# Query products of a two-layer kernel as three rounded passes of exact parts, with the heads of both sequences walked together

## The chip, the core and the metric

The kernel runs on one core of one Trainium2 chip. The metric is the device time of one execution in microseconds. The times shown are the median of three executions with the lowest and the highest beside it; the profile is of one execution.

## What is computed

Two layers, each an attention part and a feed-forward part, each followed by a residual sum and a layernorm. The change lies in the attention part of the first layer, a linear attention that reads a fixed memory, and in the way the weights of the first feed-forward part are examined. Cut to that:

```python
# x: (2, 512, 512); of the 32 heads only every 4th is used: 8 heads of 128 columns
q      = elu(x @ Wq.T + bq) + 1.0            # (b, s, 8, 128) for the 8 heads
num    = einsum('bshd,hde->bshe', q, M)      # M: (8, 128, 128)
den    = einsum('bshd,hd->bsh', q, z) + 1e-6
out    = repeat(num / den, 4 heads) @ Wo.T
x      = layernorm(x + out)
# first feed-forward: weights are ternary (-s, 0, +s), results are truncated to int8
gate, up = (x / 128) @ w_gate.T, (x / 128) @ w_up.T      # 1376 columns each
inter  = trunc(clip(silu(gate) * up * 128, -128, 127))
x      = layernorm(x + trunc(clip((inter @ w_down.T) * 128, -128, 127)))
# then a softmax attention with one head and a SwiGLU feed-forward, both untouched here
```

## The kernel before, in words

Everything lies in one function, `tile_two_layers_kernel`. A sequence of 512 rows is held as 4 row tiles of 128 x 512 (`xs[b][t]`). A scheduling layer places the instructions of TensorE (PE), VectorE (DVE), ScalarE (ACT) and the SyncE DMA queue (SP) from the program's order and its own costs; GpSimd (POOL) keeps the written order. `tc.issue_after` ties one instruction behind another. PSUM is one pool of 8 tiles of one bank each (`ps`, L68); tiles of a pool with `bufs=n` are reused in turn, and a new user waits for the readers of the old one.

**Query stage.** `transposed` (L117) and `first_rows` (L358) turn the rows with PE transposes and copy them to SBUF as `xt`. For each sequence b and head h, `queries` (L379) makes `q`: `query_products` (L350) runs 4 float32 products of 128 x 128 weights with 128 x 512 rows into one bank, ACT makes `e` (Exp, L388) and `r` (Relu, L390) from it, and DVE joins them to `q` (L392). Only head 0 of sequence 0 is done in quarters of 128 columns, as its rows arrive. All heads of sequence 0 come first, then all heads of sequence 1. Between them lie `sum_weights` (L404: three additions of output weights, on POOL for heads 0, 3, 5, 7, on DVE for the others) and `fold` (L412), which multiplies M with the summed output weights into `mw`, 128 x 512 a head; its last column is z (the denominator).

**Reading stage.** For each of the 8 row tiles, `read` (L419) runs 8 float32 products of `q` with `mw` into 8 banks (L428). ACT takes the denominators (L432), DVE inverts four at a time (L436), ACT scales three heads to `y` (L441), POOL adds them up (L445, L457), and DVE adds the other five heads to the rows (L450). `norm_a0` (L526) is the layernorm.

**Checks.** Whether the first feed-forward's weights are ternary is found out on the chip. `largest`, `over_partitions` and `scales` (L178 to L206) find the scale of gate and up from the first chunk. `check_up` (L469) divides a half chunk (128 x 512, 22 halves in 11 chunks) by the scale on ACT (L463) and compares it with the original on DVE (L210, one instruction and a read of its accumulator), counting the differences. 15 halves are checked from head 3 of sequence 1 on, 7 in the first three row tiles of the reading. `divided` (L537) runs the same division again, into tiles that the feed-forward keeps (`ts_up`), for the first `LEAD` = 6 chunks in the reading's last six row tiles. `total` and `verdict` (L214, L219) give one flag and the scale to use, `branch` (L234) loads the flag into PE registers, and `up` (L604) branches on it: 16 fp32r products per chunk and sequence (L611), with rows in two parts.

**Loads.** SP issues x of sequence 0, the query weights, x of sequence 1, M, the output weights, and then all gate and up chunks (`up_weights`, L237); `wo` tiles come from a pool of 6, so their loads wait for `sum_weights`.

The function that makes exact parts elsewhere in the kernel, in the last feed-forward:

```python
h = w * (1 - 2**-13)            # rounded to fp32r by ACT (L803)
l = (h * -4096) + 4096 * w      # DVE (L817)
d = l - h                       # DVE (L818)
```

Of the kernel before, what the change touches and what calls it, by code (L numbers as in the profile page):

```python
# [32 lines left out]
LENT = 3  # L33
TOP12 = -4096
# [4 lines left out]
def kernel(  # L39
# [179 lines left out]
    def verdict(tot, sc, name):  # L219

        k = sc.shape[-1]
        pf = psum(f"pf_{name}")
        nc.tensor.matmul(pf[:, :1], ones, tot, start=True, stop=True)
        yes = small.tile([P, 1], F32, tag="yes", name=f"yes_{name}", bufs=1)
        nc.vector.tensor_scalar(yes, pf[:, :1], 0.0, None, ALU.is_equal)
        no = small.tile([P, 1], F32, tag="no", name=f"no_{name}", bufs=1)
        nc.vector.tensor_scalar(no, pf[:, :1], 0.0, None, ALU.not_equal)
        flag = const.tile([1, 1], I32, tag=f"flag_{name}", name=f"flag_{name}")
        nc.vector.tensor_copy(flag, yes[0:1, 0:1])
        eff = const.tile([P, k], F32, tag=f"eff_{name}", name=f"eff_{name}")  # L230
        nc.vector.tensor_scalar(eff, sc, yes, no, ALU.mult, ALU.add)
        return flag, eff
# [69 lines left out]

    wqp = ctx.enter_context(tc.tile_pool(name="wqp", bufs=4))

    def query_tile(name):
        return wqp.tile([P, 2, HID], F32, tag="wq", name=name)

    with tc.tile_pool(name="a0w", bufs=1) as a0w, tc.tile_pool(name="a0", bufs=2) as a0:
# [12 lines left out]
        load_x(1)  # L321
# [4 lines left out]
        for h in range(NH):  # L326
            halves = []
            if h == 6:
                gus = up_weights(gu0_in, "0", range(1))
            for j in range(2):  # L330
                w = pair_tile(f"wo{h}_{j}")
                nc.sync.dma_start(w, wo0_in[h, :, ts(j, G // 2), :])
                halves.append(w)
            wos.append(halves)

        gus += up_weights(gu0_in, "0", range(1, len(CHUNKS)))
        nc.sync.dma_start(wqkv, wqkv_in.rearrange("(k p) f -> p k f", p=P))
        bqk = const.tile([D, 3], F32, tag="bqk", name="bqk")
        nc.sync.dma_start(bqk, bqk_in)
        nc.sync.dma_start(bv, bv_in.to_broadcast([P, D]))  # L340
        nc.sync.dma_start(wo1, wo1_in)
        nc.sync.dma_start(bo, bo_in.to_broadcast([P, HID]))

        mw = a0w.tile([D, NH, HID], F32, tag="mw", name="mw")
        nc.gpsimd.tensor_copy(mw[:, :, LAST], z)

        def query_products(pq, xt, h, at):  # L350
            for k in range(NK):
                done = nc.tensor.matmul(  # L352
                    pq[:, at], wq[h][:, k, :], xt[:, k, at],
                    start=(k == 0), stop=(k == NK - 1),
                )
            return done

        def first_rows(xt, t):  # L358

            pt = psum(f"pt_a00_{t}")  # L360
            for k in range(NK):
                done = nc.tensor.transpose(pt[:, ts(k, P)], xs[0][t][:, ts(k, P)], ident)
            pt = pt.rearrange("p (k t) -> p k t", k=NK)
            nc.scalar.copy(xt[:, :2, ts(t, P)], pt[:, :2])
            nc.vector.tensor_copy(xt[:, 2:, ts(t, P)], pt[:, 2:])
            return done

        def first_queries(pq, xt):

            done = first_rows(xt, 0)  # L370
            for t in range(NT):
                if t + 1 < NT:
                    with tc.issue_after(done.ins):
                        done = first_rows(xt, t + 1)
                with tc.issue_after(done.ins):
                    done = query_products(pq, xt, 0, ts(t, P))
            return done

        def queries(b, xt, h):  # L379

            pq = psum(f"pq_{b}_{h}")
            if b == h == 0:
                done = first_queries(pq, xt)
            else:
                done = query_products(pq, xt, h, slice(0, S))

            e = a0.tile([D, S], F32, tag="e", name=f"e_{b}_{h}")
            nc.scalar.activation(e, pq, AF.Exp, bias=bq[:, h : h + 1])  # L388
            r = a0.tile([D, S], F32, tag="r", name=f"r_{b}_{h}")
            nc.scalar.activation(r, pq, AF.Relu, bias=bq[:, h : h + 1])  # L390
            q = a0.tile([D, S], F32, tag="q", name=f"q_{b}_{h}", bufs=16)
            nc.vector.scalar_tensor_tensor(q, e, 1.0, r, ALU.min, ALU.add)  # L392
            qs[b].append(q)
            return done
# [65 lines left out]
        def ternary(eng, out, w, factor):  # L460

            if eng is nc.scalar:
                eng.activation(out, w, AF.Copy, scale=factor)  # L463
            else:
                eng.tensor_scalar(out, w, factor, None, ALU.mult)  # L465

        counts = const.tile([P, 2 * len(CHUNKS)], F32, tag="counts", name="counts")

        def check_up(c, a):  # L469
            n = CHUNKS[c][1]  # L470
            w = gus[c][:, a].rearrange("p k i -> p (k i)")
            t = a0.tile([P, NK * P], F32R, tag="t", name=f"t_{c}_{a}")
            ternary(nc.scalar, t[:, : NK * n], w, inv_up[:, a : a + 1])
            junk = a0.tile([P, NK * P], I8, tag="junk", name=f"junk_{c}_{a}", bufs=1)
            i = 2 * c + a
            compare(
                junk[:, : NK * n], t[:, : NK * n].bitcast(F32), w,
                sc_up[:, a : a + 1], counts[:, i : i + 1],
            )

        checks = [(c, a) for c in range(len(CHUNKS)) for a in range(2)]
        qs = [[], []]
        xt = xtp.tile([P, NK, S], F32, tag="xt", name="xt_a00")
        with tc.issue_after(queries(0, xt, 0).ins):
            queries(0, xt, 1)
        for h in range(2, NH):
            queries(0, xt, h)
            if h == 4:
                sum_weights(nc.gpsimd, 0)
                turn_memory()  # L490
                sum_weights(nc.vector, 1)
            elif h == 6:
                xt1 = transposed(xs[1], "a01")
                sum_weights(nc.vector, 2)
        sum_weights(nc.gpsimd, 3)
        for h in range(NH):
            queries(1, xt1, h)
            if h == 0:
# [4 lines left out]
                with tc.issue_after(copies[-1].ins):  # L503
                    mx_up = largest(
                        [gus[0][:, a].rearrange("p k i -> p (k i)") for a in range(2)], "up"
                    )
            elif h == 1:
                top_up = over_partitions(mx_up, "up")
            elif h == 2:
                sc_up, inv_up = scales(top_up, "up")  # L510
                fold(2)
# [3 lines left out]
            elif h == 3:  # L515
                fold(4)
            elif h == 5:
                fold(5)
                fold(6)
            elif h == 6:  # L520
                fold(7)
            if h >= 3:
                for _ in range(3):
                    check_up(*checks.pop(0))
        order = [(b, t) for b in range(B) for t in range(NT)]
        def norm_a0(i, steps):  # L526
# [10 lines left out]
        def divided(c, a):  # L537
            n = CHUNKS[c][1]
            if c not in ts_up:
                t = (pair_tile if c in PAIRED else query_tile)(f"tu_{c}").bitcast(F32R)  # L540
                ts_up[c] = t.rearrange("p a (k i) -> p a k i", k=NK)
                if n < P:
                    nc.gpsimd.memset(ts_up[c][:, :, :, n:].bitcast(F32), 0.0)
            ternary(nc.scalar, ts_up[c][:, a, :, :n], gus[c][:, a], inv_up[:, a : a + 1])

        PAIRED = (LEAD - 2, LEAD - 1, len(CHUNKS) - 1)
        ts_up, x2 = {}, []
# [5 lines left out]
        for i, (b, t) in enumerate(order):  # L553
            steps = read(b, t, lambda steps: norm_a0(i - 1, steps) if i else None)
            for _ in range((3, 2, 2, 0, 0, 0, 0, 0)[i]):
                check_up(*checks.pop(0))
            if i == 3:
                tot_up = total(counts, "up")
            elif i == 4:
                flag_up, eff_up = verdict(tot_up, sc_up, "up")  # L560
            if i >= len(order) - LEAD:
                for a in range(2):
                    divided(i - len(order) + LEAD, a)
# [30 lines left out]
    with tc.tile_pool(name="f0", bufs=2) as f0:  # L594
        ternary_up = branch(flag_up)
        silu_scale = const.tile([P, 1], F32, tag="silu_scale", name="silu_scale")
        nc.vector.tensor_scalar(silu_scale, eff_up[:, 0:1], 1.0 / 128.0, None, ALU.mult)
# [6 lines left out]
        def up(b, c, behind=()):  # L604
            n = CHUNKS[c][1]
            t = ts_up[c]
            pp = [psum(f"pg_f0{b}_{c}"), psum(f"pu_f0{b}_{c}")]
# [110 lines left out]

        for c in range(LEAD - 2):
            up(0, c, [cut_off[f"f00_{c - 2}"]] if c > 1 else ())  # L720
        parts, block = split(1, xt1)
# [75 lines left out]
    BIG = 4096.0  # L797
    MAIN, CROSS = 1.0 + 1.0 / BIG, 1.0 / BIG
    UPPER = 1.0 - 2.0**-13
# [34 lines left out]

    def units(tile):
        return [tile[:, i, :] for i in range(tile.shape[1])]
# [484 lines left out]
```

## Time and profile before

| what | value |
|---|---|
| time, median of 3 (lowest to highest) | 471.77 us (470.95 to 472.08) |
| profiled execution, first to last instruction (span) | 468.7 us; the page prints no other time of its own for it |
| instructions | 5727 |
| PE busy | 461.0 us (98%) |
| DVE busy | 329.5 us (70%) |
| ACT busy | 267.5 us (57%) |
| POOL busy | 115.1 us (25%) |
| granted PE clock | 0.998 |
| query stage on PE, first query product to first reading product | 6.15 to 72.32 us |
| reading stage on PE, to the first product of the feed-forward | 72.32 to 130.65 us |

How to read it: a busy PE is not a PE at its peak, since the matmuls are pipelined and their ends are modelled; the distance between the starts of equal instructions is the better measure of what one costs. A line such as `L428` is the line of the kernel. "Idle before" is the time that an engine stood still before the instructions of a group, and the name after the arrow is what ended that time.[...]

### The profile page before, as it was taken

The page shows a single profiled execution, that of the slowest core. Times are in us where ns is not written, and L with a number is a line of the kernel's source. Part 1 is how long each engine was busy: PE and PEld are TensorE (multiplying, and loading weights), DVE is VectorE, ACT ScalarE, POOL GpSimd, SP SyncE. Part 2 cuts the span into 40 slices and gives each one's busy share as a digit, 9 for nine tenths or more (in the row PEclk, how much of TensorE's full clock was granted, in tenths as well). Part 3 has the DMA queues.
Part 4 walks back from the last instruction along what each step waited for, and adds up shares of the span by engine and source line. Part 5 has one row for each costly group of instructions (what it writes and reads, how often), then busy time and mean ns, then how long its engine had stood idle before and what let it go on. Part 6 is the DMA issues. An engine that isn't in the chain of part 4 may idle for free.

```text
span 468.7 us, 5727 instructions
## 1 busy us (share of the span) xinstructions
PE 461.0 (98%) x1883; PEld 329.0 (70%) x1883; DVE 329.5 (70%) x627; ACT 267.5 (57%) x507; POOL 115.1 (25%) x144
## 2 busy tenths in 40 slices
PE   9999999999999999999999999999999999999994
PEld 8454444434478888888866567888888888888884
DVE  1165677767876767775979889895755778998632
ACT  3344799557756767456756842584645768443101
POOL 0235101566543053600357032000000000050111
PEclk9999999999999999999999999999999999999999
DMA  8989900000006500051390000000000000001001
GB/s 284 381 297 363 387 9 0 0 0 3 1 1 134 201 1 3 11 162 45 91 390 31 0 1 1 1 0 1 1 0 1 0 1 1 1 24 45 37 31 45
DMA packets 21651, 35.02 MB, mean 75 GB/s; under 512 B 9840, under 2 KB 10736, under 8 KB 21616
## 3 DMA queue, kind: packets, MB, share of 16 engines
q1 hardware_dynamic: 19616, 33.73, 20.7%
q10 hardware_dynamic: 1872, 0.56, 0.5%
q8 instruction: 22, 0.36, 0.3%
q0 software_dynamic: 128, 0.26, 0.3%
q14 instruction: 13, 0.11, 0.1%
HBM read 31.40 MB, written 2.10 MB: 71 GB/s over the span
## 4 chain that ended last, share of the span: by engine, by line
PE 71%; ACT 7%; DVE 5%; issue 3%; POOL 0%; POOLq 0%; DVEq 0%; ACTq 0%
PE pm L1111 17%; PE pg_f L611 9%; PE pu_f L611 9%; PE pc L1111 8%; PE pdm L1199 7%; PE pd_f L666 4%; PE pdc L1199 4%; DVE x L450 3%; PE pqk L893 3%; PE po L428 2%; ACT y L441 2%; ACT t L463 2%; PE pv L906 2%; PE pot L989 1%; PE po L1005 1%
## 5 line engine op out<-in xcount | busy, mean ns | idle before, releaser
L428 PE MATMUL po<-mw,q 128*128 128x512 f32 x128 | 57.1, 598 | 0.3 <-DVE mv_a L139 0.2
L352 PE MATMUL pq<-xt_a,wq 128*128 128x512 f32 (+1 forms) x152 | 56.9, 526 | 0.0
L145 POOL TENSOR_TENSOR rstd_f<-mv_f,ln_eps 128x1 f32<-128x1 f32 x15 | 4.4, 293 | 169.3 <-DVE mv_f L1214 130.2
L428 PEld LDWEIGHTS po<-mw,q 128*128 128x128 f32 x128 | 22.9, 189 | 32.1 <-issue 17.7
L352 PEld LDWEIGHTS pq<-xt_a,wq 128*128 128x128 f32 x152 | 26.2, 190 | 27.4 <-issue 25.7
L1111 PE MATMUL pm<-r,ugu 128*128 128x512 f32 x152 | 37.7, 389 | 0.0
L1111 PE MATMUL pm<-r,it_early 128*128 128x512 f32 x144 | 36.7, 392 | 0.0
L1111 PEld LDWEIGHTS pm<-r,ugu 128*128 128x128 f32 x152 | 28.5, 188 | 5.9
L1111 PEld LDWEIGHTS pm<-r,it_early 128*128 128x128 f32 x144 | 27.0, 188 | 6.1 <-issue 0.5
L169 ACT ACTIVATE ta_f<-y_f,below_half 128x512 int8<-128x512 f32 (+1 forms) x22 | 15.9, 721 | 27.0 <-DVE y_f L157 26.7
L450 DVE SCALAR_TENSOR_TENSOR x<-po,den,x 128x511 f32<-128x511 f32 x40 | 29.8, 745 | 1.9
L1121 DVE SCALAR_TENSOR_TENSOR ev_q<-pm,ev_q 128x512 f32<-128x512 f32 x27 | 18.6, 688 | 14.4 <-PE pm L1111 14.4
L637 DVE SCALAR_TENSOR_TENSOR it_f<-tb_f,ta_f 128x512 fp32r<-128x512 int16 (+1 forms) x22 | 15.4, 702 | 18.3 <-ACT tb_f L170 18.3
L445 POOL TENSOR_TENSOR y<-y,y 128x511 f32<-128x511 f32 x16 | 20.3, 1271 | 31.5 <-ACT y L441 30.8
L388 ACT ACTIVATE e<-pq,bq 128x512 f32<-128x512 f32 x16 | 11.1, 692 | 24.1 <-PE pq L352 20.6
L611 PE MATMUL pg_f<-xh,tu 128*128 128x512 f32 x88 | 24.3, 398 | 0.0
L1120 ACT ACTIVATE ev_q<-pc 128x512 f32<-128x512 f32 x27 | 16.0, 593 | 14.2 <-PE pc L1111 14.1
L465 POOL TENSOR_SCALAR td<-wd,inv_down 128x512 fp32r<-128x512 f32 x11 | 18.2, 1668 | 22.1 <-DVE inv_down L205 22.1
L611 PE MATMUL pg_f<-xl,tu 128*128 128x512 f32 x88 | 23.6, 390 | 0.0
L611 PE MATMUL pu_f<-xh,tu 128*128 128x512 f32 x88 | 23.5, 389 | 0.0
L611 PE MATMUL pu_f<-xl,tu 128*128 128x512 f32 x88 | 23.5, 389 | 0.0
L1001 ACT ACTIVATE x<-x,off_f,rstd_f 128x512 f32<-128x512 f32 x7 | 5.7, 816 | 27.7 <-POOL off_f L1000 27.7
(315 smaller groups left out, 1087.5 us busy)
## 6 DMA issues: line engine op xcount, KB each, us to landing
gu<-in_gu SPq DMA_DIRECT2D x20, 512.0 KB, 7.9
wo<-in_wo SPq DMA_DIRECT2D x16, 512.0 KB, 6.9
wd<-in_wd SPq DMA_DIRECT2D x20, 256.0 KB, 4.5
wq<-in_wq SPq DMA_DIRECT2D x8, 256.0 KB, 4.9
x<-in_x SPq DMA_DIRECT2D x7, 256.0 KB, 5.4
out<-x SPq DMA_DIRECT2D x7, 256.0 KB, 2.0
wqkv<-in_wqkv SPq DMA_DIRECT2D x1, 768.0 KB, 10.8
xt_f<-squares SPq DMA_DIRECT2D x9, 64.0 KB, 2.4
```

The source lines that it names most:

```text
L169: nc.scalar.activation(a[:n], y, AF.Relu, bias=below_half[:n])
L352: done = nc.tensor.matmul(pq[:, at], wq[h][:, k, :], xt[:, k, at], start=(k == 0), stop=(k == NK - 1),)
L428: nc.tensor.matmul(po, qs[b][h0 + j][:, ts(t, P)], mw[:, h0 + j, :], start=True, stop=True,)
L445: nc.gpsimd.tensor_add(ys[0][:, :LAST], ys[0][:, :LAST], y[:, :LAST])
L450: steps.append(nc.vector.scalar_tensor_tensor(x[:, :LAST], four[j][:, :LAST], d, x[:, :LAST], ALU.mult, ALU.add))
L465: eng.tensor_scalar(out, w, factor, None, ALU.mult)
L611: nc.tensor.matmul(pp[a], t[:, a, i % NK, :], x2[b][i], start=(i == 0), stop=(i == 2 * NK - 1),)
L666: nc.tensor.matmul(pd, inter[b][c][:, ts(t, P)], td[c].bitcast(F32R), start=(c == 0), stop=(c == last),)
L1111: nc.tensor.matmul(p, w, x, start=(left[id(p)] == begun[id(p)]), stop=(left[id(p)] == 1))
L1120: nc.scalar.activation(ev, pc, AF.Copy, scale=CROSS)
L1121: nc.vector.scalar_tensor_tensor(ev, pm, MAIN, ev, ALU.mult, ALU.add)
L1199: nc.tensor.matmul(p[:, :w], got[j // 4][1][kind][:, j % 4], down_parts[j][kind][:, cols], start=(j == 0 and kind == kinds[0]), stop=(j == ...
```

## The change

1. **Query products in parts.** The weights of a head are cut into `g`, `l`, `d` (`exact_weights`: one ACT and two DVE instructions of 128 x 512), the rows into an upper part `h`, a remainder `m` and a cross part `d` (`upper_lower`: one ACT, one DVE; `crossed`: one DVE). Instead of 4 float32 products a head takes 12 fp32r products into one bank: 8 (`g` with `h`, `l` with `m`), then ACT multiplies the bank in place by 4097 (`raise_main`), then 4 more (`d` with `d`) are added onto it. The bank then goes to Exp and Relu as before. Head 0 of sequence 0 keeps its float32 quarters; its rows are copied for that and cut into parts besides.
2. **Both sequences together.** After head 0 of sequence 0 come heads 1, 2, 3 of sequence 0, then 1, 2, 3, 0 of sequence 1, then heads 4 to 7, each for both sequences. The main passes of an item are issued ahead of the cross pass of the item before it.
3. **Room.** The parts lie in tiles of other things: the buffers of the gate and up chunks 2 to 10 (`hosts`), of `y`, `t` and three of the four `wos`. So the loads of these chunks, and the five small loads behind them, are written after the query stage (`late_loads`); chunks 0 and 1 (`EARLY` = 2) are loaded ahead of the output weights of the last heads. x of sequence 1 is loaded after the third head's weights.
4. **Checks in the reading.** Four halves are checked in the query stage, 18 with the reading. For the first 6 chunks the check uses the division that `divided` keeps, so that these 12 halves are divided once and not twice.
5. **Two verdicts.** Chunks 0 to 5 are counted for one flag, 6 to 10 for a second one (`up2`), which is made between the feed-forward's third and fourth chunk.

```diff
+    def exact_weights(w, parts):
+        g, l, d = parts
+        nc.scalar.activation(g, w, AF.Copy, scale=UPPER / BIG)
+        nc.vector.scalar_tensor_tensor(l, g.bitcast(F32), -BIG, w, ALU.mult, ALU.add)
+        nc.vector.tensor_sub(d, l.bitcast(F32), g.bitcast(F32))
+    def upper_lower(src, h, m):
+        return (
+            nc.scalar.activation(h, src, AF.Copy, scale=UPPER),
+            nc.vector.tensor_sub(m, src, h.bitcast(F32)),
+        )
+    def crossed(d, h, m):
+        return nc.vector.scalar_tensor_tensor(
+            d, m.bitcast(F32), -BIG, h.bitcast(F32), ALU.mult, ALU.add
+        )
+    def raise_main(p):
+        return nc.scalar.activation(p, p, AF.Copy, scale=BIG + 1.0)
...
-        gus += up_weights(gu0_in, "0", range(1, len(CHUNKS)))
-        nc.sync.dma_start(wqkv, wqkv_in.rearrange("(k p) f -> p k f", p=P))
+        def late_loads():
+            gus.extend(up_weights(gu0_in, "0", range(EARLY, len(CHUNKS))))
+            nc.sync.dma_start(wqkv, wqkv_in.rearrange("(k p) f -> p k f", p=P))
...
+            lows.append(upper_lower(pt, high0[:, :, ts(t, P)], low0[:, :, ts(t, P)]))
...
+        def passes(p, b, h, kinds, start):
+            todo = [(wq3[h][i][:, ts(k, D)], rows3[b][i][k]) for i in kinds for k in range(NK)]
+            for i, (w, x) in enumerate(todo):
+                done = nc.tensor.matmul(
+                    p, w, x, start=(start and i == 0), stop=(i == len(todo) - 1),
+                    skip_group_check=not start,
+                )
...
+        def main_queries(b, h):
             pq = psum(f"pq_{b}_{h}")
-            if b == h == 0:
-                done = first_queries(pq, xt)
-            else:
-                done = query_products(pq, xt, h, slice(0, S))
+            passes(pq, b, h, (0, 1), True)
+            raise_main(pq)
+            return b, h, pq
+        def cross_queries(b, h, pq):
+            if (b, h) != (0, 0):
+                passes(pq, b, h, (2,), False)
             e = a0.tile([D, S], F32, tag="e", name=f"e_{b}_{h}")
...
+        for i, (b, h) in enumerate(items):
+            begun = main_queries(b, h)
...
+            cross_queries(*held)
+            held = begun
...
+            if i > len(items) - 3:
+                for _ in range(2):
                     check_up(*checks.pop(0))
+        fold(7)
+        cross_queries(*held)
+        late_loads()
...
-            for _ in range((3, 2, 2, 0, 0, 0, 0, 0)[i]):
+            for _ in range((1, 2, 2, 3, 3, 2, 3, 2)[i]):
                 check_up(*checks.pop(0))
-            if i >= len(order) - LEAD:
-                for a in range(2):
-                    divided(i - len(order) + LEAD, a)
...
+        tot_up = total(counts_up[1], "up2")
         for c in range(LEAD - 2):
             up(0, c, [cut_off[f"f00_{c - 2}"]] if c > 1 else ())
+            if c == 2:
+                decide(1, *verdict(tot_up, sc_up, "up2"))
```

In the built program the scheduling layer moves the checks of the reading forward: all 18 comparisons stand on DVE in the first four row tiles, and five divisions of chunks 2 to 4 stand on ACT ahead of the first `y`. SP issues chunk 5 first of the late loads, then 2, 3, 4 and 6 to 10. The second flag's product stands on PE behind the feed-forward's third chunk, and its load into registers behind the fourth.

## The prediction

> **What bounds the kernel now.** I read, in this order: engine totals, busy time by stretch, the order of time on each engine, the waits. Totals and stretches (start:end, length, then busy time of each engine, instruction count in brackets, then granted clock, DMA share, GB/s):
>
> ```profile
> PE 461.0 (98%) x1883; PEld 329.0 (70%) x1883; DVE 329.5 (70%) x627; ACT 267.5 (57%) x507; POOL 115.1 (25%) x144
> 24.00:41.00 17.00, 17.00 (x59) 8.99 (x58) 11.47 (x16) 6.98 (x12) 6.43 (x4) 1.00 0.92 324
> 56.00:72.30 16.30, 16.30 (x39) 7.22 (x38) 11.62 (x28) 16.30 (x32) 0.00 (x0) 1.00 0.17 57
> 93.00:99.90 6.90, 6.90 (x17) 2.77 (x16) 4.30 (x11) 3.81 (x14) 4.13 (x6) 1.00 0.00 0
> ```
>
> PE never rests: the query stage (6.15 to 72.32) and the reading (72.32 to 130.65) are its work. ACT is full from 56 to 72, with checks. In a row tile of the reading (6.9 us) DVE is busy 4.3, POOL 4.1. The order of time (start, length, instruction) prices single steps by the distance of starts:
>
> ```profile
> 14.35 0.69 ACT L388 ACTIVATE e<-pq,bq 128x512 f32<-128x512 f32 x1 [2.17 <-PE pq L352]
> 17.78 0.69 ACT L388 ACTIVATE e<-pq,bq 128x512 f32<-128x512 f32 x1 [2.17 <-PE pq L352]
> 131.98 1.09 PE L611 MATMUL pg_f<-xl,tu 128*128 128x512 f32 x4
> 132.91 1.07 PE L611 MATMUL pu_f<-xh,tu 128*128 128x512 f32 x4
> 27.51 0.68 DVE L392 SCALAR_TENSOR_TENSOR q<-e,r 128x512 f32<-128x512 f32 x1
> 28.12 0.68 DVE L409 TENSOR_TENSOR wos<-wo 128x512 f32<-128x512 f32 x1
> ```
>
> A head of 4 float32 products comes every 3.43 us, 0.857 a product. Four fp32r products take 0.907 (131.98 to 132.89), 0.227 each. A DVE pass of 128 x 512 takes 0.60, an ACT one 0.58 from PSUM (0.61 from SBUF). DVE beside POOL:
>
> ```profile
> 248.92 1.65 DVE L818 TENSOR_TENSOR it_early<-it_early 128x512 fp32r<-128x512 f32 x1
> 243.31 11.73 POOL L967 TENSOR_TENSOR x<-x,bo 128x512 f32<-128x512 f32 x8
> 267.94 0.69 DVE L818 TENSOR_TENSOR ugu<-ugu,ugu 128x512 fp32r<-128x512 f32 x1
> 52.27 1.76 DVE L210 SCALAR_TENSOR_TENSOR junk<-t,sc_up,gu 128x512 int8<-128x512 f32 x1
> 52.03 1.45 POOL L409 TENSOR_TENSOR wos<-wo 128x512 f32<-128x512 f32 x1 [5.43 <-PE pmw L414]
> 54.16 0.75 DVE L210 SCALAR_TENSOR_TENSOR junk<-t,sc_up,gu 128x512 int8<-128x512 f32 x1
> ```
>
> The same subtraction takes 0.69 alone and 1.65 while POOL adds; the comparison 0.75 and 1.76.
>
> [...] the blocked DVE step ends about 0.5 us behind POOL's. The DVE sum L450, which has one input in PSUM, keeps to 0.73 to 0.75 throughout, POOL busy or not. [...] The trace: 0.857 / 0.227 = 3.8. [...]
>
> **The change part by part.** R is the start of the reading on PE, 72.32 before.
>
> *PE, query stage.* 15 heads go from 3.43 to 12 x 0.227 = 2.72 us: -0.71 x 15 = -10.65, so R = 61.7 if nothing waits. Transposes and folds are the same in number.
>
> *ACT, query stage.* Added: 15 raises x 0.58 = 8.7; 8 weight cuts x 0.61 = 4.9; uppers 4 x 0.6 = 2.4 for sequence 0, for sequence 1 two more passes than the two copies they replace, 1.2. Sum +17.2. Gone: 17 of the 21 divisions before 72.3, -10.4. With 16 x (0.58 x 2) = 18.6 for e and r, 8 folds x 0.78 = 6.2, 2.5 of copies and the four remaining divisions, ACT has some 48 us of work in the 55 between 6 and 61: hidden. PE needs a raise only behind the next head's eight products (1.8 us), and ACT needs about 1 for it. An in-place pass in PSUM is not shown; nearest row L1120 (PSUM to SBUF, 0.59). From 0.5 to 0.7 it stays hidden; I take 0.58.
>
> *DVE, query stage.* Added: 16 weight passes, 8 cross parts, 4 remainders and 2 net for sequence 1, 30 x 0.60 = 18; gone 12 comparisons x 0.85 = 10.2. Sum +7.8, to about 44 us in 55. But it is crowded at the start. First rows: the copies that the float32 quarters wait for now stand behind two uppers and a weight cut on ACT (1.8 us, where ACT idled 1.2 and 1.0 ahead of these copies) and behind two remainders on DVE. Walking both queues with these durations, the first fp32r product starts at about 11.8, where head 1 started at 10.4: +1.4 us. Lower bound 0.5 (weights of head 1 land early and all is hidden), upper 2.5. From there to 24 us DVE has no gap: what it makes there, weight parts, cross parts and the remainders of sequence 1, PE takes at once.
>
> *POOL against DVE there.* POOL's first summing began at 20.5, when its weights had landed; the loads ahead of it hold the same bytes, so it begins there again, 2.35 + 1.26 us. In it DVE has two-SBUF passes that PE waits for. DVE loses up to 3.6; some of it is spent in remainders, which read PSUM, and the PE queue has about 1 us in hand: +1.8, bounds 0 and 3.6. Later sums (10.9 us of POOL) meet a DVE with about 13 us free: nothing. R = 61.7 + 1.4 + 1.8 = 64.9.
>
> *Reading.* PE alone needs 64 x 0.857 + 16 transposes (1.9) + 0.2 = 57.0; before took 58.3. DVE per row tile: 5 x 0.66 + 0.6 + two inversions and small ones 0.6 = 4.5. The 18 comparisons x 0.85 now all stand in the first four tiles, 11 us of them (13 comparisons) in tiles 1 to 3 and the end of tile 0. DVE then needs 10.5, 7.8, 7.9, 6.0 us, against 6.9 of PE. POOL reads SBUF 4.1 us of 6.9, and blocks a comparison until its addition ends: walked through, about eight of the 18 are caught, 0.2 to 1.1 us each, 3.5 in all. The bank of head 7 of tile t is needed by head 7 of tile t+1, which PE reaches at R + 12.9, 19.9, 26.8, 33.7; DVE frees it at R + 14.6, 23.2, 31.7, 39.1. So PE loses up to 39.3 - 33.7 = 5.6 us by tile 4; behind that DVE needs less than PE. 57.0 + 5.6 = 62.6, with 0.4 for other short stops 63.0: +4.7 on before's 58.3. Without the blocking 2.5, with every comparison caught in full 8.
>
> *Late loads.* Chunks 2 to 10 (4.6 MB) leave the query stage, whose DMA was never the bound. Chunk 2's tile comes free when the cross pass of (0, 7) is done, R - 1.8. A 256 KB load into an idle queue took 3.0; 256 KB more at the 391 GB/s of the page add 0.7: an estimate of 3.7, so R + 2.0. ACT's first division, queued ahead of three denominators and all y, has its turn at R + 2. Nothing more is lost, but there is no cover: every microsecond of lateness moves y, and the bank of head 0 has only half a microsecond.
>
> *ACT in the reading.* 3.6 us a tile, 18 divisions x 0.61 = 11, four casts: some 43 in 63. The 10 divisions of `divided` that stood in the reading go; they were under PE.
>
> *Second verdict.* One product of one column (0.14 on PE), one register load (0.1 at the flag of down, 204.64) behind a further 3.6 us of products, five small DVE steps under PE: +0.2. The remainder of the kernel is as it was, shifted.
>
> Sum: -10.65 + 1.4 + 1.8 + 4.7 + 0.2 = -2.6 us. The two walks lean to the late side: the scheduler's order lets POOL wait for DVE as well as DVE for POOL, and I charged DVE every time. I take 0.6 off and predict -3.2. The span is 468.7, to 465.5. The median lies 3.1 above that span; I keep this: 468.6.
>
> **The rivals.** (1) *DVE keeps up*: comparisons slip between POOL's additions, start hidden by half. -10.65 + 0.7 + 0.6 + 1.5 + 0.2 = -7.6, 464.1. For it: the L450 passes are never blocked, DVE was 62% busy in a tile. Against: 11 us of comparisons against three tiles with 2.4 us free each. (2) *No change*: the upper ends of start and blocking, -10.65 + 2 + 2.5 + 5.5 + 0.2 = -0.5, 471.3. (3) *Slower: the late loads hold ACT.* In the reading's first tile five divisions stand in ACT's queue ahead of the first y. If chunk 2 lands at R + 8, as loads did in the full queue of before (7.9 us median from issue), and the others 1.3 us apart, y, the denominators and through them all DVE sums start 6 us later, in front of DVE's full three tiles: -3.2 + 6 = +2.8, 474.6. It decides from about 3.2 us of lateness. Against: the queue is empty then. (4) The change does not do what it says, the fp32r passes costing more with changing weights: L611 changes weights at every product too, so I give it nothing.
>
> **How the numbers follow.** About 0.3%, 1.4 us, is what a measurement of this kernel can tell from no change. My case, -1.4 to -5.5: 0.42. Rival 1: 0.30. Rival 2: 0.16. Rival 3: 0.12. Faster 0.72, same 0.16, slower 0.12. The range: 463.3 (below rival 1 by 0.8) to 472.2 (above rival 2 by 0.9) leaves out rival 3 and a little at the low end.
>
> **What would show it.** Right: first fp32r product near 11.8; the reading starting at 63.5 to 66; comparisons of 1.0 to 1.8 us under POOL's additions in tiles 1 to 3; reading products waiting for DVE sums there, none after tile 4; 62 to 64 us of reading. Wrong: a gap on ACT ahead of the first division (rival 3), a reading of 59 us (rival 1), raises that PE waits for late in the query stage, or a start of the reading behind 68.

## The result, and the profile after

The changed kernel took 474.37 us (median of 7 runs, 471.96 to 474.64), the kernel before 470.95 beside it (7 runs, 470.31 to 472.08): a ratio of 1.0056, 95% interval 1.0037 to 1.0074. It is slower by half a per cent. 468.6 was predicted, in a range up to 472.2. The profiled execution is one of the quick ones: span 470.5, its own time 472.3.

The totals first, then two stretches of the changed kernel (start:end, length, busy time and instruction count of PE, PE's weight loads, DVE, ACT, POOL; then granted clock, DMA share, GB/s) that answer to those shown of before:

```profile
PE 455.3 (97%) x1945; PEld 341.9 (73%) x1945; DVE 358.7 (76%) x663; ACT 277.2 (59%) x524; POOL 127.3 (27%) x144
```

```profile
24.00:41.00 17.00, 17.00 (x77) 13.45 (x77) 15.37 (x18) 11.48 (x20) 6.41 (x3) 1.00 0.70 245
93.00:99.90 6.90, 5.91 (x13) 2.00 (x12) 6.69 (x17) 4.66 (x14) 4.10 (x4) 1.00 0.00 0
```

PE is busy for 5.7 us less, and no longer all of it back to back: in the row tile of the reading at 93 it stands for a seventh of the time, and DVE is full. The larger hole lies in the query stage. PE in order of time there (start, length, instruction; in brackets how long it stood still before it, and what ended that):

```profile
32.65 1.07 PE L502 MATMUL pq<-xh_a,host_t 128*128 128x512 f32 x4
33.55 1.07 PE L502 MATMUL pq<-xl_a,host_t 128*128 128x512 f32 x4
34.46 1.07 PE L502 MATMUL pq<-host,host_y 128*128 128x512 f32 x4
35.37 1.98 PE L502 MATMUL pq<-host,host_t 128*128 128x512 f32 x8
...
43.14 3.33 PE L502 MATMUL pq<-host,host_y 128*128 128x512 f32 x12
50.05 0.38 PE L202 MATMUL pbc_up<-dg_up,ones 2*128 2x2 f32 x2 [3.58 <-DVE dg_up L195]
...
50.92 2.01 PE L502 MATMUL pq<-xh_a,host_t 128*128 128x512 f32 x4
52.73 1.91 PE L502 MATMUL pq<-xl_a,host_t 128*128 128x512 f32 x4
```

Twelve fp32r products come in 2.7 us from start to start, as reckoned (32.65 to 35.37). At 46.47 PE falls idle and stands for 3.58 us in front of a product of two columns: the one that spreads the checks' scale over the partitions. Behind the stop four products take 1.8 us from start to start, twice their 0.91: the granted clock fell.

```profile
46.50:50.00 3.50, 0.00 (x0) 0.00 (x0) 3.46 (x7) 2.36 (x5) 0.16 (x1) 1.00 0.93 266
50.00:52.00 2.00, 1.95 (x7) 1.31 (x8) 1.97 (x6) 0.48 (x2) 1.83 (x1) 0.91 1.04 364
52.00:54.00 2.00, 2.00 (x6) 1.53 (x5) 2.00 (x2) 1.90 (x3) 2.00 (x1) 0.50 0.24 94
54.00:56.00 2.00, 2.00 (x7) 1.52 (x6) 2.00 (x2) 1.33 (x4) 1.66 (x2) 0.73 0.00 0
```

The low clock costs 2 x (0.09 + 0.50 + 0.27) = 1.7 us. What PE waits for is the scale's second small step, `dg_up`. DVE ahead of it:

```profile
42.64 2.87 DVE L317 SCALAR_TENSOR_TENSOR host_t<-host_t,wq 128x512 fp32r<-128x512 f32 x1
45.58 2.17 DVE L538 TENSOR_TENSOR wo<-wo,wo 128x1024 f32<-128x1024 f32 x1
47.67 0.68 DVE L540 TENSOR_TENSOR wos<-wo 128x512 f32<-128x512 f32 x1
...
48.87 0.68 DVE L318 TENSOR_TENSOR host<-host_t,host_t 128x512 fp32r<-128x512 f32 x1
49.47 0.27 DVE L193 TENSOR_REDUCE top_up<-pmx_up 2x1 f32<-2x128 f32 x1
49.78 0.22 DVE L195 TENSOR_SCALAR dg_up<-ident,top_up 2x2 f32<-2x2 f32 x1
```

A weight step that takes 0.6 elsewhere took 2.87, a sum of output weights 2.17 where others took 1.2. POOL in the same time:

```profile
42.20 2.76 POOL L538 TENSOR_TENSOR wo<-wo,wo 128x1024 f32<-128x1024 f32 x1 [5.28 <-DVE host_y L318]
45.04 1.62 POOL L540 TENSOR_TENSOR wos<-wo 128x512 f32<-128x512 f32 x1
```

The weight step (42.64 to 45.51) ends half a microsecond behind POOL's sum (42.20 to 44.96), and the next DVE sum ends behind POOL's next one (45.04 to 46.66): these two DVE steps lost 2.3 + 1.0 us, about what PE stood still. It is the taking of turns that the prediction's pairs from the kernel before show (a subtraction of 0.69 and 1.65 us, a comparison of 0.75 and 1.76), at a place where it had charged nothing.

So the reading starts at 68.31, not at 64.9 (before 72.32). It takes 62.99 us, and 63.0 were predicted. One more wait, of 0.94 us, lies far behind: a layernorm step ahead of the last transposes (234.10), behind two small steps of POOL for it that took 2.08 and 1.48 instead of 0.55. It is in this profile only; the others of this document don't show it.

### The profile page after: what moved, and what is told of

It reads as the page before. It is cut to its first block, busy times and chain, and to the rows that moved or that the text cites. A ratio compares the mean times of both kernels' runs of the same rounds, so it can differ in the third digit from the quotient of the medians.

```text
span 470.5 us, 5923 instructions
## 1 busy us (share of the span) xinstructions
PE 455.3 (97%) x1945; PEld 341.9 (73%) x1945; DVE 358.7 (76%) x663; ACT 277.2 (59%) x524; POOL 127.3 (27%) x144
## 4 chain that ended last, share of the span: by engine, by line
PE 68%; DVE 5%; issue 2%; POOL 1%; ACT 1%; POOLq 0%; DVEq 0%
PE pm L1242 17%; PE pg_f L744 9%; PE pu_f L744 8%; PE pc L1242 8%; PE pdm L1330 7%; PE pdc L1330 4%; PE pqk L1024 3%; PE po L559 3%; DVE x L581 2%; PE pv L1037 2%; PE pot L1120 1%; PE po L1136 1%; PE psc L1062 1%; PE pd_f L799 1%; POOL rstd_f L146 1%
## 5 line engine op out<-in xcount | busy, mean ns | idle before, releaser
L559 PE MATMUL po<-mw,q 128*128 128x512 f32 x128 | 58.8, 603 | 3.2 <-DVE x L581 1.9
L146 POOL TENSOR_TENSOR rstd_f<-mv_f,ln_eps 128x1 f32<-128x1 f32 x15 | 6.9, 458 | 168.1 <-DVE mv_f L1345 130.3
L576 POOL TENSOR_TENSOR y<-y,y 128x511 f32<-128x511 f32 x16 | 22.8, 1427 | 22.3 <-ACT y L572 21.7
L538 POOL TENSOR_TENSOR wo<-wo,wo 128x1024 f32<-128x1024 f32 x4 | 15.4, 3849 | 21.5 <-DVE q L524 6.4
L524 DVE SCALAR_TENSOR_TENSOR q<-e,r 128x512 f32<-128x512 f32 x16 | 14.5, 906 | 8.2 <-ACT r L522 8.2
L799 PE MATMUL pd_f<-td,it_f 128*128 128x512 f32 x88 | 20.3, 389 | 0.0
```

The lines of the kernel that those rows point to most:

```text
L559: nc.tensor.matmul(po, qs[b][h0 + j][:, ts(t, P)], mw[:, h0 + j, :], start=True, stop=True,)
L576: nc.gpsimd.tensor_add(ys[0][:, :LAST], ys[0][:, :LAST], y[:, :LAST])
L799: nc.tensor.matmul(pd, inter[b][c][:, ts(t, P)], td[c].bitcast(F32R), start=(c == 0), stop=(c == last),)
```

## The experiments

The profiled execution of each (start and length of the reading are PE's; a ratio is to the kernel before in the same runs):

| run | stop at the scale, us | reading starts | reading takes | span | median of runs | ratio, 95% interval |
|---|---|---|---|---|---|---|
| before | none | 72.3 | 58.3 | 468.7 | 470.95 | |
| as changed | 3.58 | 68.3 | 63.0 | 470.5 | 474.37 | 1.0056 (1.0037 to 1.0074) |
| e1_scale_later | 2.84 | 67.6 | 63.0 | 468.7 | 470.77 | 1.0005 (0.9991 to 1.0018) |
| e2_no_pool | none | 63.1 | 63.1 | 464.1 | 466.01 | 0.9903 (0.9889 to 0.9917) |
| e3_no_cmp | 3.65 | 68.4 | 58.8 | 465.4 | 467.75 | 0.9959 (0.9940 to 0.9978) |
| e4_spread | 5.73 | 71.5 | 61.7 | 473.5 | 474.35 | 1.0068 (1.0056 to 1.0081) |
| e5_sums_dve | none | 62.5 | 62.6 | 462.9 | 465.88 | 0.9911 (0.9898 to 0.9923) |
| e6_no_y_adds | 5.66 | 70.8 | 58.0 | 466.6 | 468.54 | 0.9964 (0.9952 to 0.9977) |
| e7_scale_first | 3.63 | 68.3 | 62.9 | 469.4 | 471.48 | 1.0038 (1.0025 to 1.0050) |
| e8_dve_spread | none | 62.7 | 64.4 | 464.8 | 466.85 | 0.9922 (0.9908 to 0.9935) |
| c1_before_dve | none | 72.3 | 58.0 | 468.5 | 470.67 | 1.0003 (0.9995 to 1.0012) |
| e11_both | none | 63.5 | 58.6 | 459.9 | 461.08 | 0.9791 (0.9775 to 0.9807) |
| e10_lent2 | none | 63.0 | 60.3 | 461.1 | 462.85 | 0.9836 (0.9822 to 0.9849) |
| c2_after_again | 3.70 | 68.4 | 62.7 | 469.3 | 472.91 | 1.0050 (1.0037 to 1.0064) |
| e12_sum_first | 5.92 | 71.2 | 63.9 | 472.8 | 474.09 | 1.0071 (1.0058 to 1.0085) |

### The stop in the query stage

**Put the scale's product later.**

```diff
             elif i == 9:
-                top_up = over_partitions(mx_up, "up")
                 fold(2)
             elif i == 10:
-                sc_up, inv_up = scales(top_up, "up")
                 fold(3)
...
             elif i == 11:
+                top_up = over_partitions(mx_up, "up")
                 fold(4)
             elif i == 12:
+                sc_up, inv_up = scales(top_up, "up")
                 fold(5)
```

> Only the place of the scale chain changes: its transpose stands two items later in the query stage, its product (the one that PE waited 3.58 us for at 46.5) two items later too. Main theory (this one product, standing in PE's order in front of work that was ready, holds PE while DVE is late, and the rest of the loss is the lower granted clock of 0.5 to 0.9 from 50 to 56, which costs 1.7 and comes only from the stop): no stop at 46.5, clock 1.00 up to 60, the reading starts at 63.0 (62.5 to 64) instead of 68.3, time about 469.0. Rival A (the stop alone goes, the low clock has another cause): start 64.7, slow products still near 51. Rival B (another DVE product takes its place, since DVE stays as late as it is): a stop of 2 to 3.5 us before weights or folded sums between 45 and 52, start 66 to 68, time 472 or more.

PE of this kernel, in order of time:

```profile
52.87 0.85 PE L502 MATMUL pq<-host,host 128*128 128x512 f32 x3
56.55 0.35 PE L202 MATMUL pbc_up<-dg_up,ones 2*128 2x2 f32 x2 [2.84 <-DVE dg_up L195]
...
57.40 2.31 PE L502 MATMUL pq<-xh_a,host_y 128*128 128x512 f32 x4
```

The stop at 46.5 went, and came again at 53.7, under the same product, with the same slow products behind it; the start moved by 0.8 only. PE worked from 46.5 to 53.7 on products that in the changed kernel stood behind this one: there, ready work waited behind a product that could not start. POOL's next sum (49.93 to 52.52, and 1.6 of its second part) stretched the two DVE steps ahead of the scale there as well. So the main theory was wrong in taking this product's place for the cause; it was right about the clock, which fell where the stop was. Rival B is near in the start (66 to 68), not in the time: 470.77, where it had 472 or more. It is DVE's lateness that has to go.

**Take POOL's sums away.** Part of the computation is left out, as the expectation says.

```diff
             w, w1 = wos[h]
-            eng.tensor_add(w, w, w1)
             s = a0.tile([D, HID], F32, tag="wos", name=f"wos{h}", bufs=4)
+            if eng is nc.gpsimd:
+                nc.scalar.copy(s, w[:, 0, :])
+                nc.scalar.copy(s[:, :1], w1[:, 0, :1])
+                wos[h] = s
+                return
+            eng.tensor_add(w, w, w1)
             eng.tensor_add(s, w[:, 0, :], w[:, 1, :])
```

> Leaves out POOL's additions of the output weights of heads 0, 3, 5 and 7: ACT copies the first of the four blocks instead (0.6 us each), so nothing reads SBUF on POOL in the query stage; the order on DVE and PE stays. Main theory (POOL's two-input additions and DVE's two-input steps take turns on SBUF and stretch each other): the stretched DVE steps (1.8 to 2.9 us at 33 to 54) go back to 0.6 to 0.7, the scale's two small steps come 3 us or more earlier, the stop at 46.5 is gone or under 0.7 though its product stands where it stood, start of the reading 63.0 (62.5 to 64.2), time about 469. Rival (DVE has too much work of its own, or waits for late output weights): its steps short but the stop still 2 us or more, start 66 or later, time 472 or more.

DVE of this kernel, the same steps:

```profile
38.36 0.68 DVE L317 SCALAR_TENSOR_TENSOR host_t<-host_t,wq 128x512 fp32r<-128x512 f32 x1
...
41.05 1.23 DVE L544 TENSOR_TENSOR wo<-wo,wo 128x1024 f32<-128x1024 f32 x1 [0.57 <-DMA wo<-in_wo]
42.81 0.69 DVE L318 TENSOR_TENSOR host<-host_t,host_t 128x512 fp32r<-128x512 f32 x1 [0.53 <-PE pq L502]
43.42 0.27 DVE L193 TENSOR_REDUCE top_up<-pmx_up 2x1 f32<-2x128 f32 x1
43.80 0.22 DVE L195 TENSOR_SCALAR dg_up<-ident,top_up 2x2 f32<-2x2 f32 x1
```

`dg_up` comes 6 us earlier, in an unchanged order; the step of 2.87 takes 0.68. No stop, the clock at 1.00 throughout, start 63.1 where 63.0 was expected, and a ratio of 0.9903 in place of 1.0056. The time, 466.0, is 3 us under the 469 expected, which was reckoned from the median of the changed kernel; most of its runs were longer than the profiled one (see the spread of its times below). DVE still waited for late output weights (0.57 here, 2.06 at 35.4), without harm.

**Give POOL's sums to DVE.** Nothing is left out.

```diff
-                sum_weights(nc.gpsimd, 0)
+                sum_weights(nc.vector, 0)
...
-                sum_weights(nc.gpsimd, 3)
+                sum_weights(nc.vector, 3)
...
-                sum_weights(nc.gpsimd, 5)
+                sum_weights(nc.vector, 5)
...
-                sum_weights(nc.gpsimd, 7)
+                sum_weights(nc.vector, 7)
```

> All sums of the output weights stand on DVE; POOL reads no SBUF in the query stage, and nothing is left out. DVE gets 4 x (1.15 + 0.6) = 7 us more of its own. Main theory (not the amount of DVE's work but POOL's additions between its steps held PE): no step of DVE over 1.3 us in the query stage, no stop at the scale's product above 0.7 us, start of the reading 63.1 to 64.5 as without POOL's sums at all, time 466.0 to 467.5. Rival (DVE's work is too much, the runs without sums were quick because work was left out): stops of 2 us or more before weights, folded sums or the scale, start 66 or later, time 469 or more.

One stretch of the query stage, of the changed kernel and then of this one:

```profile
20.00:50.00 30.00, 26.47 (x116) 20.51 (x114) 28.27 (x33) 21.82 (x40) 14.71 (x6) 1.00 0.75 257
```

```profile
20.00:50.00 30.00, 30.00 (x130) 23.09 (x130) 29.83 (x47) 24.49 (x45) 0.00 (x0) 1.00 0.81 291
```

DVE ends 47 instructions there instead of 33 and is busy for 29.8 us of 30, and PE doesn't stand still once. So DVE's own work was not too much. From the first fp32r product (11.06) to the reading it takes 51.5 us; in the changed kernel (from 11.66) 56.7. The difference, 5.2, is the stop with its low clock. This version beats the kernel before by 0.9% (and the changed one by 1.4%, the ratios divided). As a control the same four lines were edited in the kernel before:

> The kernel before, with all sums of the output weights on DVE; nothing is left out. A control for the version with the change and all sums on DVE (465.9). Theory (there DVE had room and PE waited for none of its steps that POOL stretched): no effect, start of the reading 72.0 to 72.6, time 469.8 to 470.8. Rival (taking the sums off POOL is worth 2 us or more whatever the query products are): 468.5 or less.

It made no difference there (1.0003), so the gain belongs to the query stage as changed, in which PE had to wait for DVE.

### Two groups of times

The twelve runs of the changed kernel (with those of c2_after_again) spread from 471.1 to 474.6: three up to 472.3, five from 472.5 to 473.4, four from 474.3 on. They can be read as two groups, but the numbers leave no clear gap at 472.4. In two profiles (e4_spread, e6_no_y_adds), with the query stage's order unedited, the stop was 5.7. What differs is who comes first near 49.8: `dg_up`, or POOL's last sum. Both orders were forced. First the sum was put behind the step:

```diff
+                nc.gpsimd.tensor_copy(fill[0:2, 2:4], top_up)
                 sum_weights(nc.gpsimd, 7)
```

> As changed, but POOL's last sum of output weights (head 7) is made to wait for the scale's second small step on DVE, by a copy of 2 x 2 of it. In the profile of the changed kernel that sum began 0.17 us after this step (step 0.22 us, stop 3.58 us); in the run with comparisons spread it began 0.08 us before it, and the step took 2.28 us, the stop 5.73. Theory (the times of the changed kernel lie in two groups, 472.1 and 474.4, since these two steps race for SBUF): all runs lie in the lower group, 471.5 to 472.5, the stop is 3.6. Rival (the groups come from elsewhere, such as a late layernorm step at 233): times as before, 472 to 474.6, median 474.

Four of six runs lay at 471.15 to 471.57, two at 472.47 and 473.04. The changed kernel itself ran later, in another group of runs:

> The changed kernel itself, for its times beside those of the version in which POOL's last sum stands behind the scale's step (471.15 to 473.04, median 471.48). Theory (the race of these two steps makes the upper group): half or more of the runs at 473.3 to 474.7, the others near 472, median 473 or more. Rival (the two versions are alike): median under 472.

One run of five at 471.13, four at 472.52 to 473.24, and none at 473.3 or more, where the theory had half of them. Against the kernel before, the ratios are 1.0038 and 1.0050, with intervals that overlap. That leans to the theory, with too few runs to hold it. So the opposite order was forced, by letting `dg_up` take its 2 x 2 identity from a tile that POOL copies once the sum's weights are there:

```diff
...
+                for half in wos[7]:
+                    nc.gpsimd.tensor_copy(fill[0:2, 5:7], half[0:2, 0, 0:2])
+                nc.gpsimd.tensor_copy(fill[0:2, 2:4], ident[0:2, 0:2])
+                sum_weights(nc.gpsimd, 7)
+                dg = small.tile([2, 2], F32, tag="dg2", name="dg_up", bufs=1)
+                nc.vector.tensor_scalar_mul(dg, fill[0:2, 2:4], top)
+                sc_up, inv_up = scales(dg, "up")
```

> As changed, but the scale's second small step on DVE needs a 2 x 2 tile that POOL copies right ahead of its last sum of output weights, after that sum's weights have landed. So the sum starts first, as it did in the run with comparisons spread (step 2.28 us, stop 5.73). Theory (who starts first decides between the two groups of times of the changed kernel): the step takes about 2.2 us, the stop is 5.5 to 6, the low clock lasts longer, the reading starts at 70.8 to 71.5, and all times lie in the upper group, median 473.3 to 475. Rival (the groups come from elsewhere): median under 473, or times in two groups as before.

DVE's step and POOL's sum of this kernel, then PE's product:

```profile
49.80 2.28 DVE L654 TENSOR_SCALAR dg_up<-fill,top_up 2x2 f32<-2x2 f32 x1 [0.17 <-POOL fill L651]
```

```profile
49.73 2.33 POOL L538 TENSOR_TENSOR wo<-wo,wo 128x1024 f32<-128x1024 f32 x1
```

```profile
52.14 0.58 PE L202 MATMUL pbc_up<-dg_up,ones 2*128 2x2 f32 x2 [5.92 <-DVE dg_up L654]
```

A start 0.07 us behind POOL's turns a step on four numbers from 0.22 into 2.28 us; the stop becomes 5.92, the reading starts at 71.2, and all five runs lie at 473.57 to 474.60. This order makes the upper end of the times. That it makes every long run is not shown. The granted clock of whole runs is a hint: it is 0.994 or 0.995 in the profiled runs with a stop of 2.8 to 3.7 us, 0.988 to 0.990 in those with 5.7 to 5.9, and 0.988 to 0.991 in nine of the twelve runs of the changed kernel. But one of these nine took only 471.96, and the two longer runs of e7_scale_first, 472.5 and 473.0, have 0.991 though POOL's sum stood behind the step. What made those two long is open.

### The reading

**No comparisons.**

```diff
-            compare_up(a0, c, a, t)
+            if c < EARLY:
+                compare_up(a0, c, a, t)
```

> Leaves out the 18 comparisons that stand in the reading (their counts stay zero); the divisions on ACT and all loads stay. Main theory (comparisons on DVE in the first four row tiles lengthen the reading): the reading takes 58.3 to 58.8 us instead of 63.0, its start unchanged at 68.3, time about 469.9. Rival (late loads and the divisions on ACT hold the first tiles): the reading stays at 61 or more, time 472.5 or more.

The reading took 58.8. So the late loads and ACT's divisions, which this kernel keeps, cost at most half a microsecond; rival 3 of the prediction is out. In the changed kernel ACT waited for a late load, chunk 2, for 0.73 us:

```profile
70.82 0.72 ACT L344 ACTIVATE tu<-gu,inv_up 128x512 fp32r<-128x512 f32 x1 [0.73 <-DMA gu<-in_gu]
```

**Comparisons spread over all tiles.**

```diff
-                check_up(*checks.pop(0))
+                check_up(*checks.pop(0), steps[-1])
```

Inside `check_up`, `compare_up` then stands under `tc.issue_after(behind.ins)`.

> Each comparison of the reading is held behind the last sum of its own row tile, so 1 to 3 stand in each tile instead of all 18 in the first four. By tile DVE then has 4.5 us of its own and 0.9 to 2.6 of comparisons against 6.9 us of PE. Main theory (it is the crowding of the first tiles that PE waits for): the reading takes 59.5 (58.8 to 61), time about 471. Rival (POOL's additions catch the comparisons wherever they stand, each costing what it costs now): 62 to 63, time 473.5 or more.

It took 61.7, between the two expectations; the query stage, whose order is the same, happened on the long stop, and so the time is that of the changed kernel. The gain was 1.3 us, with new stops before transposes in the late tiles. Together with the sums on DVE, and with none in the last tile:

```diff
-            for _ in range((1, 2, 2, 3, 3, 2, 3, 2)[i]):
+            for _ in range((2, 3, 3, 3, 3, 2, 2, 0)[i]):
-                check_up(*checks.pop(0))
+                check_up(*checks.pop(0), steps[-1])
```

> Both cures with nothing left out: all sums on DVE, and the comparisons of the reading held behind the last sum of their own tile, 2, 3, 3, 3, 3, 2, 2, 0 by tile, so that none stands in the last tile. Spread as 1, 2, 2, 3, 3, 2, 3, 2 the reading took 61.7 us instead of 63.0, 1.3 of it in stops before the transposes of its last tiles. Theory (each cure keeps what it brought alone): start 63.1 to 64.5, reading 60.5 (59.5 to 61.5), time 464 (463 to 465.5). Rival (each tile pays for its comparisons wherever they stand): reading 62.5 or more, time 466.5 or more.

The reading took 64.4, worse than unspread (62.6 in e5_sums_dve). Spreading gained 1.3 in one layout and lost 1.8 in the other, so it is no cure; whether crowding is the cause, the next run decides. Comparisons and POOL's addition to x, DVE and then POOL, in one tile of e8_dve_spread:

```profile
106.93 0.74 DVE L211 SCALAR_TENSOR_TENSOR junk<-t,sc_up,gu 128x512 int8<-128x512 f32 x1
...
108.26 1.10 DVE L211 SCALAR_TENSOR_TENSOR junk<-t,sc_up,gu 128x512 int8<-128x512 f32 x1
...
109.47 1.56 DVE L211 SCALAR_TENSOR_TENSOR junk<-t,sc_up,gu 128x512 int8<-128x512 f32 x1
```

```profile
106.97 1.84 POOL L588 TENSOR_TENSOR x<-x,y 128x511 f32<-128x511 f32 x1 [0.80 <-DVE x L581]
108.77 3.40 POOL L576 TENSOR_TENSOR y<-y,y 128x511 f32<-128x511 f32 x2
```

A comparison (106.93) meets POOL's addition to x, which then takes 1.84 instead of 1.27, and each of the next two waits for an addition of POOL's. The tile before shows the same (comparisons of 1.09 and 1.57).

**No additions on POOL in the first four tiles.** Part of the computation is left out, as the expectation says.

```diff
-                        if ys:
+                        if ys and (b, t) >= (1, 0):
                             nc.gpsimd.tensor_add(
...
-            else:
+            elif (b, t) >= (1, 0):
                 nc.gpsimd.tensor_add(x[:, :LAST], x[:, :LAST], ys[0][:, :LAST])
```

> Leaves out POOL's additions in the first four row tiles of the reading (three lent heads are not added to those rows); ACT still writes their y, DVE's work and all 18 comparisons stay. Theory of the prediction (4.7 of the reading are 2.5 of DVE's own comparisons and 2.2 of waiting for POOL's additions): comparisons at 0.75, the reading takes 60.8 (60.2 to 61.3), time about 472. Rival (the wait for POOL is all of it): 58.5 to 59.5, time 470.5. Rival (DVE's own work is all of it): 62.5 or more, time 474.

The comparisons of the reading, as groups (instruction, count, busy time, mean ns, idle before), in the changed kernel and then here:

```profile
L211 DVE SCALAR_TENSOR_TENSOR junk<-t,sc_up,gu 128x512 int8<-128x512 f32 (+1 forms) x10 | 11.2, 1118 | 0.2
L211 DVE SCALAR_TENSOR_TENSOR junk<-tu,sc_up,gu 128x512 int8<-128x512 f32 x8 | 6.7, 839 | 1.1 <-ACT tu L344 0.9
```

```profile
L211 DVE SCALAR_TENSOR_TENSOR junk<-t,sc_up,gu 128x512 int8<-128x512 f32 (+1 forms) x10 | 7.0, 702 | 0.0
L211 DVE SCALAR_TENSOR_TENSOR junk<-tu,sc_up,gu 128x512 int8<-128x512 f32 x8 | 6.0, 746 | 0.6 <-ACT tu L344 0.4
```

The reading took 58.0 us with all 18 comparisons still in the first four tiles, so neither their crowding nor DVE's own work on them costs PE anything. Nor do POOL's additions alone: e3_no_cmp keeps them, without comparisons, at 58.8. Only both together cost the 5.0 us, and the comparisons themselves lost 17.9 - 13.0 = 4.9 to the wait for POOL. (The time of this run contains the long stop of 5.66, so it is no measure of the reading.) Both cures together:

> All sums on DVE, and POOL's additions in the first four row tiles of the reading left out (three lent heads are not added to those rows). Theory (both losses are POOL and DVE taking turns on SBUF and nothing else of the change costs PE more than the start of 1.4): start 62.5, reading 58.1, so the feed-forward starts at 120.6, time 461.4 (460.5 to 462.3). Rival (the reading then starts earlier than late loads allow, and takes over as bound): the reading takes 59.5 or more, time 463 or more.

The start was 63.5, the reading 58.6, the time 461.08. The start is 1.0 later than in e5_sums_dve because the first fp32r product began at 12.03 instead of 11.06; from there to the reading it is 51.5 us again, as in e2_no_pool and e10_lent2. The reading is 0.5 over the expectation. So no third loss larger than that stands behind the two.

**One head less on POOL.** On top of the sums on DVE, nothing left out:

```diff
-                    if h0 + j < LENT:
+                    if h0 + j < (LENT if b else LENT - 1):
```

> All sums on DVE; in the first four row tiles of the reading two heads are lent to ACT and POOL instead of three, so POOL reads SBUF 2.5 us of a tile instead of 3.8 to 4.1, and DVE has one sum from PSUM more (0.66). Nothing is left out. Theory (POOL's share decides): fewer comparisons caught, the reading takes 61 to 62, time 465. Rival (DVE's own work then decides, 8.6 us in tiles 1 to 3): the reading takes 63 or more, time 466.3 or more.

The comparisons of the reading in this kernel, as groups:

```profile
L211 DVE SCALAR_TENSOR_TENSOR junk<-t,sc_up,gu 128x512 int8<-128x512 f32 (+1 forms) x10 | 7.9, 794 | 0.0
L211 DVE SCALAR_TENSOR_TENSOR junk<-tu,sc_up,gu 128x512 int8<-128x512 f32 x8 | 6.3, 785 | 1.2 <-ACT tu L344 1.1
```

DVE has 4 x 0.66 = 2.6 us more to do in these tiles, its comparisons take 3.7 less than in the changed kernel (14.2 for 17.9), and the reading takes 60.3. At 462.85 us, a ratio of 0.9836 (0.9822 to 0.9849), this is the best version with the whole computation, faster than both kernels.

## Why the prediction was wrong

The span was predicted at 465.5 and came out at 470.5.

- **PE, query stage (-10.65).** Right: 12 products in 2.7 us, and in e5_sums_dve the start is 62.5, for 72.32 - 10.65 + 1.4 = 63.1. Nothing speaks for rival 4. (The two lines that the prediction took the price from begin at 131.98 and 132.91, 0.93 apart; the pairs behind them are 0.91 apart, and its 0.227 stands.) The raise in place took 0.58 to 0.60, and PE shows no further step for it: 180 products in 15 heads, 12 each.
- **Start (+1.4).** Right: the first fp32r product began at 11.66, for 11.8. It moved between 11.06 and 12.03 in versions that begin alike.
- **POOL's first summing (+1.8).** It cost PE nothing: POOL's first sum took 4.69 us from 18.33, and DVE lost 2.1 (two cross parts, from 21.86, took 3.42 us instead of 1.28), but PE had no stop before 46.5. Error: -1.8.
- **"Later sums (10.9 us of POOL) meet a DVE with about 13 us free: nothing."** This step failed: it put the later sums at nothing because DVE had free time over the whole stage (13 us, or 11 by the prediction's own 44 of 55). From 20 to 50 us DVE was busy for 28.27 of 30, and in its order the scale stood behind a weight step and a sum that POOL stretched by 2.3 and 1.0 us, with PE's product waiting in PE's order for it. Stop 3.58 and low clock 1.7: error +5.3. With the sums off POOL (e2_no_pool, e5_sums_dve) both are gone. The start of the reading is thus 64.9 - 1.8 + 5.3 - 0.1 = 68.3. It is past 68, which the prediction had named as a sign that it was wrong.
- **Reading (63.0).** The sum was right to a tenth by luck, as its parts were not. "Without the blocking 2.5" is wrong: without it the reading takes 58.0 to 58.6 (e6_no_y_adds, e11_both), for 58.3 of before. DVE's own share was nothing, and the blocking was all of it.
- **The lean of -0.6.** It went the wrong way: error +0.6.
- **Late loads, second verdict.** Right: ACT waited 0.73 us for chunk 2, at R + 2.5 for R + 2.0; the feed-forward's part is 0.2 longer but for the layernorm wait of 0.94, which the prediction had not reckoned with. (The 391 GB/s that it took from the page is the rate of one stretch, 41 to 56 us; the page's highest is 390.)

Together 3.4 + 0.6 + 0.9 = 4.9 of the 5.0 us. The median stands 3.9 above the profiled span, where 3.1 was taken: most runs list a granted clock as low as the profiles with the longer stop do, and the profiled run does not. Of the rivals, the slower one was right in its sign and wrong in its place: the loads that it named came in time. No case had a stop of PE in the query stage.

## What to carry to other kernels

Free time of an engine is counted between the step that blocks it and the step that another engine waits for, never over a stage: here a DVE busy for 29.8 us of 30 without POOL's sums cost PE nothing, and one busy for 28.3 beside them cost it 5.3. Before a POOL step with SBUF inputs is left beside a DVE queue that PE feeds on, look for the smallest step in that queue that an in-order product waits for (here `dg_up`, 0.22 us, and a stop of 3.58). Where DVE and POOL share work on SBUF, moving some of POOL's to DVE can be faster though DVE gets more to do (here 465.88 us for 474.37).

## What the runs showed of the hardware

- The taking of turns lengthens both sides: POOL's sum of 128 x 1024 took 2.35 us alone and up to 5.15 (e1_scale_later, at 30.05); DVE steps of 0.7 took up to 2.88 (the same run, at 42.77). The sums that took longest got in late. One of the changed kernel, POOL first, then DVE:

```profile
31.16 4.07 POOL L538 TENSOR_TENSOR wo<-wo,wo 128x1024 f32<-128x1024 f32 x1 [6.44 <-DVE q L524]
```

```profile
32.28 0.68 DVE L318 TENSOR_TENSOR host<-host_t,host_t 128x512 fp32r<-128x512 f32 x1
32.88 0.68 DVE L184 TENSOR_REDUCE mx_up<-gu 128x1 f32<-128x512 f32 x1
33.47 2.30 DVE L524 SCALAR_TENSOR_TENSOR q<-e,r 128x512 f32<-128x512 f32 x1
```

POOL's sum ends at 35.23, its full 2.35 after the reduction began at 32.88, the first DVE step behind its start that has no second input in SBUF; then it holds the next DVE step until 35.77. The sum of 5.15 likewise ends 2.35 after such a reduction began (32.85), the one at 18.33 2.36 after a remainder with an input in PSUM began (20.66). It is not always so: the sum at 42.20 got in between two DVE steps with two inputs.
- A step on 2 x 2 numbers is caught as a large one is (0.22 in the changed kernel, 2.28 in e12_sum_first). DVE's sums with one input in PSUM kept to 0.74 (the mean of 40) in the changed kernel's reading.
- The half rate, a granted clock of 0.50, stands behind every stop at the scale, the shortest of them 2.84 us (e1_scale_later). It lasted some 3.4 us at the stops of 2.84 to 3.65 (51.7 to 55.1 in the changed kernel) and some 6.8 us at those of 5.66 to 5.92, part of it still inside the stop. The fall came 0.5 to 1.6 us after PE had begun again behind the stops of 2.84 to 3.70. Both ends of that are of the same kernel: 1.6 in the profile of the changed kernel, 0.5 in c2_after_again, an estimate from two products (50.39) that took 1.87 us there and 1.02 at 55.74. A stop of 3.58 cost 5.3.
